# Two groups' affine, residual and norm moved from the last stage into the attention before it, and the folding of its weights moved into the experts

## Chip, cores and metric

The kernel runs on one core of a Trainium2 chip (trn2). The metric is the device time of one launch in microseconds; the time of a kernel is the median of its runs. The compute engines are TensorE (PE), VectorE (DVE), ScalarE (ACT) and GpSimd (POOL). SyncE (SP) issues most of the DMAs, ACT's queue the others.

## The reference, cut to what matters

A batch of sequences with 128 channels passes through four layers, each made of an attention-like mixer and a feed-forward part. In the kernel it is 32 tiles of 128 rows, held in `xt`, and worked on in eight groups of four tiles (`TG = 4`, `GT = 512` rows). Three parts matter here:

- the feed-forward part of layer 2: eight experts (gate, up, silu, down), of which each row takes the best two;
- the mixer of layer 3: four selective state-space (mamba) layers in a row, each with a projection, a short convolution, a recurrence over time with 16 states, a gate, a projection out, and a residual and normalisation behind it;
- the feed-forward part of layer 3: two layers of local attention with rotary positions and a gated MLP.

Between the last two stands the normalisation's affine and the outer residual, followed by the norm before the last part:

```
x = x_norm * w + b            # affine of the norm behind the mixer
x = x + x6                    # residual: what entered layer 3
x7 = x                        # residual of the last part
x = (x - mean(x)) / sqrt(var(x) + eps)
```

The convolution before the recurrence (4 taps) and the input projection are both linear, so the kernel multiplies the taps into the projection's matrix beforehand. This is the "folding": for each of the four layers a tile of 128 x 1024 taps times the projection (128 x 256, repeated four times).

## The kernel before, in words

The stages run one after another, each with its own pools: `l01`, `l2_attn`, `l2_ffn` (the experts), `l3_attn` (four mamba layers x eight groups = 32 items), `l3_ffn` (two layers x eight groups = 16 items).

**Who sets the order.** In `l2_ffn` the tile framework schedules the instructions by its own estimates. In `l3_attn` and `l3_ffn` nothing is issued while the code runs: a `Recorder` (L335) takes every operation with a key, which is its place in a written plan plus a shift for its kind; `Recorder.run` (L529) then does a list scheduling by a cost model of its own, with the smallest key first among what is ready, and issues the planned order, which is kept on each engine. An operation recorded in one stage can't be issued in another. All recorded operations bear line L299 in the profile, so they are told apart by their tiles.

**Folding (`ssm_fold`, L1511).** SP loads the taps (`cw`, one row broadcast to 128 partitions, 512 KB written) and the projection (`inx`, 128 KB), POOL multiplies. `l3_attn` (L1861) begins with four folds, one for each layer, each stored to a DRAM tile `wxd`, and then `weights(0)`, which loads the first layer's pack `w_L3a` (128 x 968) and reads its folded matrix back into `wx`. Both rings have two buffers; the weights of layer l+1 are loaded while the last group of layer l runs. The folds' operands and `w_L3a` go through SP's queue, behind the stores of `x6`.

**Items of the attention (`ssm_run`, L1758).** Item i is layer i/8, group i%8, with key origin `i * L`, `L = 32`. Per item POOL does eight multiplies of 128 x 2048 (`sb<-sw,sB`, the input of the scans), one of `sw`, two of `scq` and two operations of 128 x 512 for the norm (`xt<-so,smv` and `xt<-xt,srs`); DVE does 32 scans; PE transposes the results back and sums them over the states.

**The last stage (`l3_ffn`, L2072).** It loads its constants (`L3f`, `L3mask` on ACT's queue, `w_ln` on SP's), clears the parts of some tiles on POOL, and records 16 items with keys from `L3F` (L2162): `aff`, `hT`, `qkv`, `rot`, `tr`, `max`, `mn`, `sc`, `val` and the nine of `tail` (`wo` to `x`). For layer 0, `l3_affine` (L2206) does for each group what stands in the block above: SP loads `xo` (from `x6`), three operations on POOL (times w, plus b, plus `xo`), a store of `x7` on SP, statistics on DVE, Ln and Exp on ACT, and two more operations on POOL (minus mean, times 1/sigma). `l3_hT` transposes the result on PE, `l3_qkv` projects it with weights that are split into two parts: `l3_weights` (L2171) loads them in pieces (`w_in`, 128 x 512), ACT casts the upper part, POOL subtracts to get the rest (`wqkv_lo`, `w_lo`), and POOL then scales the rotary table `tab` from `w_L3f`.

`l3_affine` and the changed functions are in this listing.

Of the kernel before, what the change touches and what calls it, by code (L numbers as in the profile page):

```python
# [11 lines left out]
F32 = mybir.dt.float32  # L12
# [10 lines left out]
P = 128  # L23
NSEQ = 16
SEQ = 256
NTOK = NSEQ * SEQ
D = 128
# [629 lines left out]
class Ker:  # L657
    def __init__(self, ctx, tc, packs, dram, x_in, out):
        self.ctx, self.tc = ctx, tc
        self.nc = Engines(tc)  # L660
        self.packs, self.dram = packs, dram
        self.x_in, self.out = x_in, out
        nc = self.nc
        self.cp = ctx.enter_context(tc.tile_pool(name="cp", bufs=1))
        self.wp = ctx.enter_context(tc.tile_pool(name="wp", bufs=1))
        self.sp = self.sp0 = ctx.enter_context(tc.tile_pool(name="sp", bufs=2))

        self.xd = ctx.enter_context(tc.tile_pool(name="xd", bufs=1, space=bass.MemoryType.DRAM))
        self.x6 = self.xd.tile([P, NTOK // P, D], F32, name="x6")
        self.c = self.load("const")  # L670
        self.ident = self.cv("ident")
        self.xt = self.cp.tile([P, NTOK // P, D], F32, name="xt")
        xv = x_in.rearrange("b (k p) d -> p (b k) d", p=P)
        for g in range(4):
            s = slice(8 * g, 8 * g + 8)
            nc.sync.dma_start(self.xt[:, s], xv[:, s])

    def load(self, name, pool=None):
        pk = self.packs[name]
# [828 lines left out]
        r[0] += 1  # L1508
        return r[1][(r[0] - 1) % len(r[1])]

    def ssm_fold(self, tag, wx):  # L1511

        nc = self.nc
        t = self.ring("sb", [P, 4, GT], 7).rearrange("p n t -> p (n t)")
# [240 lines left out]
        ),  # L1755
    }

    def ssm_run(self, items, begin, norm, finish, N, after=None):  # L1758

        nq, n = N // 4, len(items)  # L1760
        L = 8 * nq
        pl = self.plan
        ev = []

        def at(t, f, *a):
            ev.append((t, len(ev), f, a))

        self.rec.shift = {k: pl["slot"] * v for k, v in pl["shift"].items()}

        for i, item in enumerate(items):  # L1770
# [12 lines left out]
            at(o + pl["src"], self.ssm_src, S)  # L1783
            if after:
                at(o + pl["src"] + 0.1, after, item)
            for c in range(2):
                at(o + pl["u"][c], self.ssm_in, S, c)
            for k in range(2):
                at(o + pl["z"][k], self.ssm_in, S, 2 + k)
            at(o + pl["silu"], self.ssm_silu, S)  # L1790
            at(o + pl["xp"], self.ssm_xp, S)
            for k in range(4):
                at(o + pl["dt"][k], self.ssm_dt, S, k % 2, k > 1)
            for k in range(3):
                at(o + pl["soft"][k], self.ssm_soft, S, k)
            for q in range(nq):
                s = o + 8 * q
                at(o + pl["bl"][q], self.ssm_bload, S, q)
                for c in range(2):
                    at(s + 4 * c + pl["b"][0], self.ssm_b, S, q, c)  # L1800
                for j in range(8):
                    at(s + j - 2.6, self.ssm_exp, S, q, j)
                    at(s + j, self.ssm_scan, S, q, j)
                    t = s + 9 + j
                    at(t + 0.2, self.ssm_tr, S, q, j)
                    at(t + 0.5, self.ssm_ev, S, q, j)
                    if j % 2:
                        at(t + 1.3, self.ssm_y, S, q, j // 2)
            e = o + L
            for k in range(2):  # L1810
                at(e + pl["ys"][k], self.ssm_ys, S, k)
                at(e + pl["gt"][k], self.ssm_gt, S, k)
            at(e + pl["out"], self.ssm_out, S)
            for t in pl["fin"]:
                at(e + t, step, "f", finish, item, S)
        ev.sort(key=lambda e: e[:2])
        for t, _, f, a in ev:
            self.rec.key, self.rec.kind = pl["slot"] * t, f.__name__[4:] or a[0]
            f(*a)
        self.nc.record(None)  # L1820
        self.rec.penalty = pl["pen"]
        self.rec.run(pl["ahead"])
        self.last_act = self.nc.scalar.last

    def l2_attn(self):
        nc, pk = self.nc, self.packs["L2a"]
        with ExitStack() as st:
# [9 lines left out]
            self.ssm_fold("L2", wx)  # L1837
            A, dd = self.ssm_decay(W, 8)
            b = self.sbank()
            for c in range(2):  # L1840
# [20 lines left out]
    def l3_attn(self):  # L1861
        nc = self.nc
        with ExitStack() as st:
# [3 lines left out]
            self.rec.apart, self.rec.switch, self.rec.rate = True, 0.09, 2330.0  # L1867
            self.rec.key = -1e6
            nc.record(self.rec)
            wd = self.dp.tile([4, P, 1024], F32, name="wxd", bufs=1)  # L1870
            for l in range(4):
                wx = self.ring("s4", [P, 2, GT], 2).rearrange("p a b -> p (a b)").rearrange("p (k e) -> p k e", k=4)
                self.ssm_fold(f"L3{l}", wx)
                nc.sync.dma_start(wd[l], wx.rearrange("p k e -> p (k e)"))
            cur = [self.xt[:, TG * g : TG * (g + 1)] for g in range(NG)]
            live = {}

            def weights(l):
                pk = self.packs[f"L3a{l}"]
                wt = self.ring("w_L3a", [P, pk.width], 2)  # L1880
                nc.sync.dma_start(wt, self.dram[f"L3a{l}"])
                wx = self.ring("wx", [P, 4, 256], 2)
                nc.sync.dma_start(wx.rearrange("p k e -> p (k e)"), wd[l])
                W = lambda n: pk.view(wt, n)
                live[l] = [W, wx]

# [16 lines left out]
            def after(item):  # L1903
                l, g = item
                if g == NG - 1 and l < 3:
                    weights(l + 1)

            weights(0)
            self.ssm_run([(l, g) for l in range(4) for g in range(NG)], begin, norm, finish, 16, after)


    def l2_ffn(self):
        nc, pk = self.nc, self.packs["L2m"]
        with self.tc.tile_pool(name="moe", bufs=2) as tp, self.tc.tile_pool(name="moew", bufs=1) as wp:
# [22 lines left out]
            for g in range(NG):  # L1937
                nxt = self.moe_route(g + 1, S[g + 1], W) if g + 1 < NG else none()
                prev = None
                for e in range(9):  # L1940
# [6 lines left out]
                    prev = (g, e, h, S[g], dw[e]) if e < 8 else None  # L1947
                    if e >= 2:
                        next(nxt, None)
                for _ in nxt:  # L1950
                    pass

# [119 lines left out]
    def l3_ffn(self):  # L2072
        nc = self.nc
        with ExitStack() as st:
# [5 lines left out]
            wm = self.load("L3mask", stat)  # L2080
            self.M = lambda n: self.packs["L3mask"].view(wm, n)
            self.wln = stat.tile([P, 2, D], F32, name="w_ln")
            nc.sync.dma_start(self.wln.rearrange("p a d -> p (a d)"), self.dram["L3ln"])
            self.epst = stat.tile([P, 1], F32, name="epst3")
            nc.vector.memset(self.epst, EPS)
            x7 = self.xd.tile([P, NTOK // P, D], F32, name="x7")
            ring = lambda n, f: [f(i) for i in range(n)]

            def shifted(i):
# [36 lines left out]
            for l in range(2):  # L2126
                at(pl["L"] * NG * l + pl["w"], "w", lambda l=l: live.update({l: self.l3_weights(l)}))
                for g in range(NG):
                    o = pl["L"] * (NG * l + g)
                    S = dict(i=NG * l + g, l=l, q=[], v=[], vx=[], live=live, xs=self.xt[:, TG * g : TG * (g + 1)])  # L2130
                    part = slice(TG * g, TG * (g + 1))
                    if l == 0:
                        at(o + pl["aff"], "aff", self.l3_affine, S, self.x6[:, part], x7[:, part])
                    at(o + pl["hT"], "hT", self.l3_hT, S)
                    for k in range(TG):
# [25 lines left out]

    L3F = dict(  # L2162
        L=46.0, w=-14.0, aff=-8.0, hT=4.0, qkv=8.0, tr=18.0, mid=(27.0, 41.0), tail=(66.0, 73.0, 75.0, 77.0, 81.0, 85.0, 88.0, 92.0, 96.0),
        pen=819.1, ahead=200.0, shift={
            "aff": -5.1, "gate": -11.4, "gelu": 394.9, "hT": -62.4, "ln": 137.7, "max": -127.7, "mn": -410.9,
            "nrm": 69.1, "qkv": -128.2, "rot": -171.0, "sc": 39.2, "stick": 33.1, "tr": -158.4, "up": 14.7,
            "val": -79.2, "w": 39.8, "w2": 358.8, "wo": -262.4, "x": 1.0, "yT": 26.4,
        },
    )

    def l3_weights(self, l):  # L2171
        nc = self.nc
        pk, p3 = self.packs[f"L3f{l}"], self.packs[f"L3w{l}"]
        wt = self.ring("w_L3f", [P, pk.width], 2)
        nc.sync.dma_start(wt, self.dram[f"L3f{l}"])
        parts = []
        for nm, bufs in (("wqkv", 1), ("w1", 2)):
            n = p3.items[nm][2][0]
# [2 lines left out]
            for j in range(0, n, 512):  # L2181
# [311 lines left out]
def kernel(ctx, tc, packs, dram, x_in, out, stages=STAGES):  # L2493
    k = Ker(ctx, tc, packs, dram, x_in, out)
    for s in stages:
        with tc.tile_pool(name="w_" + s, bufs=1) as k.wp, tc.tile_pool(name="ps_" + s, bufs=8, space=PSUM) as k.ps:
            k.nc.in_order(k.IN_ORDER.get(s, ""))
            getattr(k, s)()
    k.store()


# [19 lines left out]
```

## Time and profile before

| what | value |
|---|---|
| runs | 3915.74, 3921.61, 3924.74 us |
| median | 3921.61 us |
| the profiled execution's own time | 3928.12 us |
| its span in the profile | 3926.3 us |
| mean granted PE clock | 0.932 |
| PE busy | 3373.7 us (86%) |
| DVE busy | 3142.2 us (80%) |
| ACT busy | 2631.6 us (67%) |
| POOL busy | 2431.3 us (62%) |

The stages as the trace shows them: the experts from about 1318 to 1645 us, the attention of layer 3 from there to 3213, the last stage to the end at 3926. The experts take 39.7 us a group, the attention 46.8 us an item, the last stage 40.4 us an item.

The profile's second part cuts the span into 40 slices of 98 us; a digit is the busy share of an engine in tenths. PEclk is the clock that TensorE was granted, in tenths of its full rate. A line of a timeline gives start and busy time in us, the engine, the operation with its output and inputs, how many of them stand in a row, and in brackets how long the engine was idle before and what it waited for. In a table of windows each row is a stretch of time with the busy time of PE, PE's weight loads, DVE, ACT and POOL (the count of instructions in brackets), then the granted clock, the share of DMA time and GB/s.

### The profile page before, as it was taken

What the parts mean: (1) busy time and instruction counts of PE and PEld (TensorE: products, weight loads), DVE (VectorE), ACT (ScalarE), POOL (GpSimd) and SP (SyncE); (2) the same over time, 40 slices, a digit from 0 to 9 for tenths busy, and PEclk for the clock granted to TensorE, in tenths of its full rate; (3) what the DMA queues carried; (4) which work ended last, traced back from release to release, by engine and by line L of the source; (5) the groups of instructions that cost most, each with busy time, mean ns of one, the idle gap of its engine ahead of it and who ended that gap; (6) DMA issues with size and microseconds to landing.
All of it is one profiled execution on the core that took longest, in us unless ns stands there. A gap on an engine that the chain in (4) does not pass through costs nothing.

```text
span 3926.3 us, 77843 instructions
## 1 busy us (share of the span) xinstructions
PE 3373.7 (86%) x31425; PEld 2258.7 (58%) x31425; DVE 3142.2 (80%) x5420; ACT 2631.6 (67%) x4291; POOL 2431.3 (62%) x1163
## 2 busy tenths in 40 slices
PE   7863147666799899879999999999999968999998
PEld 4321034445355688736666666666666646777776
DVE  4699867556488677559999999999999968888874
ACT  4542024343587443369999999999999967777766
POOL 3454412211387200179999999999999978665553
PEclk9876568878899999899999999999999989999999
DMA  1012121321121100222222232222222220000001
GB/s 47 1 37 36 35 49 34 60 34 27 50 74 67 37 6 9 75 78 99 91 102 88 89 110 89 99 89 94 99 89 98 89 87 28 12 12 6 6 11 37
DMA packets 113833, 224.10 MB, mean 57 GB/s; under 512 B 53536, under 2 KB 84896, under 8 KB 94368
## 3 DMA queue, kind: packets, MB, share of 16 engines
q1 hardware_dynamic: 110736, 214.35, 17.8%
q8 instruction: 247, 4.05, 0.4%
q10 hardware_dynamic: 2736, 4.78, 0.4%
q14 instruction: 114, 0.93, 0.1%
HBM read 195.10 MB, written 21.76 MB: 55 GB/s over the span
## 4 chain that ended last, share of the span: by engine, by line
PE 46%; ACT 17%; DVE 4%; issue 2%; DMA 1%; POOL 1%; POOLq 0%; SPq 0%; DVEq 0%; ACTq 0%
PE spb L299 14%; PE fb L299 10%; PE shT L299 8%; ACT abuf L299 5%; ACT shs L299 5%; PE gu L299 5%; PE sy L299 4%; PE md L299 3%; PE fp L299 2%; ACT L299 2%; ACT su L299 2%; ACT s L299 1%; DVE mx L299 1%; PE mx L299 1%; DVE qr L299 1%
## 5 line engine op out<-in xcount | busy, mean ns | idle before, releaser
L299 POOL TENSOR_TENSOR sb<-sw,sB 128x2048 f32<-128x2048 f32 x288 | 1333.5, 4655 | 52.3 <-PE shT L299 49.8
L299 DVE TENSOR_TENSOR_SCAN sb<-abuf,sb 128x512 f32<-128x512 f32 x1152 | 1323.4, 1203 | 44.3 <-ACT abuf L299 22.9
L299 ACT ACTIVATE abuf<-sdl,sA 128x510 f32<-128x510 f32 x1152 | 780.9, 702 | 46.6 <-DVE sb L299 43.1
L299 PEld LDWEIGHTS shT<-w_const,sb 128*128 128x128 f32 x4608 | 595.0, 194 | 284.9 <-ACT shs L299 118.5
L299 PE MATMUL shT<-w_const,sb 128*128 128x128 f32 x4608 | 667.8, 283 | 29.6 <-ACT shs L299 16.0
L299 ACT COPY shs<-shT 128x512 f32<-128x512 f32 x920 | 517.7, 597 | 49.8 <-PE shT L299 35.4
L299 PE MATMUL sy<-shs,scq 128*32 128x256 f32 x4608 | 360.0, 390 | 0.2 <-DVE shs L299 0.2
L299 PE MATMUL spb<-ypad,wx 128*128 128x512 f32 x640 | 304.8, 613 | 6.1 <-ACT su L299 3.0
L299 DVE TENSOR_REDUCE mx<-fp 128x8 f32<-128x1024 f32 x160 | 193.7, 1218 | 105.9 <-PE fp L299 104.2
L299 POOL TENSOR_TENSOR qn<-qn,qr 128x512 f32<-128x512 f32 x128 | 163.8, 1281 | 172.6 <-DVE qr L299 114.9
L299 ACT ACTIVATE pt<-fp 128x1024 f32<-128x1024 f32 x96 | 97.2, 1024 | 181.8 <-PE fp L299 177.6
L299 ACT ACT_TABLE_LOAD x148 | 189.9, 1283 | 25.0 <-PE fb L299 18.2
L299 POOL TENSOR_TENSOR yn<-xt,nmv 128x512 f32<-128x512 f32 x23 | 24.0, 1043 | 285.8 <-DVE nmv L299 239.3
L299 PE MATMUL gu<-my,gu 128*128 128x512 f32 x768 | 197.6, 406 | 1.9 <-ACT gu L299 1.5
L299 PEld LDWEIGHTS spb<-ypad,wx 128*128 128x128 f32 x640 | 116.1, 194 | 142.6 <-issue 115.3
L299 ACT ACTIVATE mh<-gu,w_moe 128x512 f32<-128x512 f32 x128 | 88.2, 689 | 158.0 <-PE gu L299 135.6
L299 DVE COPY shs<-shT 128x512 f32<-128x512 f32 x232 | 152.4, 678 | 46.2 <-PE shT L299 31.0
L299 PE MATMUL fb<-wqkv_hi,hT 128*128 128x512 f32 x384 | 162.4, 441 | 4.5 <-ACT hT L299 1.3
L299 PEld LDWEIGHTS sy<-shs,scq 128*32 128x32 f32 x4608 | 100.2, 108 | 113.1 <-issue 44.7
L299 PEld LDWEIGHTS gu<-my,gu 128*128 128x128 f32 x768 | 140.9, 190 | 32.7 <-ACT gu L299 1.6
L299 POOL TENSOR_TENSOR g8k<-soft,gz 128x2048 f32<-128x2048 f32 x28 | 102.9, 3684 | 71.3 <-DVE gw L299 52.3
L299 PE MATMUL spb<-sxs,w_L3a 80*128 80x512 f32 x256 | 139.3, 626 | 7.0 <-DVE s L299 2.6
(377 smaller groups left out, 7172.6 us busy)
## 6 DMA issues: line engine op xcount, KB each, us to landing
sB<-scr SPq DMA_DIRECT2D x144, 1024.0 KB
l1scr<-qk SPq DMA_DIRECT2D x24, 256.0 KB
QS<-l1scr SPq DMA_DIRECT2D x96, 64.0 KB
KS<-l1scr SPq DMA_DIRECT2D x96, 64.0 KB
pks<-pk SPq DMA_DIRECT2D x4, 1152.0 KB
rec<-pks SPq DMA_DIRECT2D x8, 576.0 KB
x<-xt SPq DMA_DIRECT2D x16, 256.0 KB
xo<-x SPq DMA_DIRECT2D x16, 256.0 KB
```

The lines of the kernel that those rows point to most:

```text
L299: r = f(*a, **kw)
```

## The change

It has five parts.

1. The folding and the first layer's weights go into the experts' stage. A pool `held` is opened before `l2_ffn` and closed behind `l3_attn`; it holds `w_L3a` and `wx` of layer 0. After expert 4 of group 0, 1, 2 and 3 the fold of layer 0, 1, 2 and 3 is written into `l2_ffn` (for layer 0 the load of `w_L3a` too), through `fold_in` and `fold_out` with one buffer each; layers 1 to 3 go to `wxd` as before. `l3_attn` then has nothing to fold, and layer 0 nothing to load.
2. `ssm_run` gets a hook `end`: for the last layer's groups 0 and 1 it records `l3_affine` with the keys `n * L + 1` and `n * L + 2`, that is, at the end of the plan of `l3_attn`. `w_ln` is loaded for it in that stage. `x7` is made at the start.
3. `l3_ffn` leaves `aff` out for the groups that have had it.
4. In `l3_ffn` `w_ln` is loaded on ACT's queue, and `w_L3f` behind the pieces of `wqkv`.
5. `L3F` has another `pen`, `ahead` and other shifts.

```diff
+        self.x6, self.x7 = (self.xd.tile([P, NTOK // P, D], F32, name=n) for n in ("x6", "x7"))
+        self.affined = set()
...
+    def hold(self):
+        self.held = ExitStack()
+        p = self.held.enter_context(self.tc.tile_pool(name="held", bufs=1))
+        self.held_w = p.tile([P, self.packs["L3a0"].width], F32, name="w_L3a_h")
+        self.held_x = p.tile([P, 4, 256], F32, name="wx_h")
+        self.wd = self.xd.tile([4, P, 1024], F32, name="wxd")
+        self.folded = set()
+
+    def fold(self, l, t, wx):
+        nc = self.nc
+        if not l:
+            nc.sync.dma_start(self.held_w, self.dram["L3a0"])
+        self.ssm_fold(f"L3{l}", wx if l else self.held_x, t)
+        if l:
+            nc.sync.dma_start(self.wd[l], wx.rearrange("p k e -> p (k e)"))
+        self.folded.add(l)
...
@@ ssm_run
+            if end and i < n - NG + 2 and i >= n - NG:
+                at(n * L + 1.0 + i - n + NG, self.ssm_end, end, item)
@@ l3_attn
-            wd = self.dp.tile([4, P, 1024], F32, name="wxd", bufs=1)
-            for l in range(4):
+            for l in sorted(set(range(4)) - self.folded):
                 wx = self.ring("s4", [P, 2, GT], 2).rearrange("p a b -> p (a b)").rearrange("p (k e) -> p k e", k=4)
-                self.ssm_fold(f"L3{l}", wx)
-                nc.sync.dma_start(wd[l], wx.rearrange("p k e -> p (k e)"))
+                self.fold(l, self.ring("sb", [P, 4, GT], 7).rearrange("p n t -> p (n t)"), wx)
+            self.ring("w_L3a", [P, self.packs["L3a0"].width], 1)
+            self.ring("wx", [P, 4, 256], 1)
+            for nm, t in (("w_L3a", self.held_w), ("wx", self.held_x)):
+                self.rings[nm] = [0, [t] + self.rings[nm][1]]
...
+            self.wln = self.stat.tile([P, 2, D], F32, name="w_ln4")
+            nc.sync.dma_start(self.wln.rearrange("p a d -> p (a d)"), self.dram["L3ln"])
+
+            def end(item):
+                g = item[1]
+                part = slice(TG * g, TG * (g + 1))
+                self.l3_affine(dict(xs=self.xt[:, part]), self.x6[:, part], self.x7[:, part])
+                self.affined.add(g)
@@ l2_ffn
+                    if e == 4 and g < 4:
+                        ft = wp.tile([P, 1280], F32, name="fold_in", bufs=1)
+                        self.fold(g, ft, wp.tile([P, 4, 256], F32, name="fold_out", bufs=1))
@@ l3_ffn
-            nc.sync.dma_start(self.wln.rearrange("p a d -> p (a d)"), self.dram["L3ln"])
+            nc.scalar.dma_start(self.wln.rearrange("p a d -> p (a d)"), self.dram["L3ln"])
-                    if l == 0:
+                    if l == 0 and g not in self.affined:
                         at(o + pl["aff"], "aff", self.l3_affine, S, self.x6[:, part], x7[:, part])
@@ L3F
-        pen=819.1, ahead=200.0, shift={
-            "aff": -5.1, "gate": -11.4, "gelu": 394.9, "hT": -62.4, "ln": 137.7, "max": -127.7, "mn": -410.9,
-            "nrm": 69.1, "qkv": -128.2, "rot": -171.0, "sc": 39.2, "stick": 33.1, "tr": -158.4, "up": 14.7,
-            "val": -79.2, "w": 39.8, "w2": 358.8, "wo": -262.4, "x": 1.0, "yT": 26.4,
+        pen=505.2, ahead=178.0, shift={
+            "aff": 36.5, "gate": 16.1, "gelu": 498.3, "hT": -76.4, "ln": 96.6, "max": -100.6, "mn": -467.4, "nrm": 45.2,
+            "qkv": -122.9, "rot": -191.8, "sc": 27.2, "stick": 43.1, "tr": -157.5, "up": 26.4, "val": -84.6, "w": 57.6,
+            "w2": 422.8, "wo": -123.9, "x": 203.0, "yT": 71.8,
@@ l3_weights
-        wt = self.ring("w_L3f", [P, pk.width], 2)
-        nc.sync.dma_start(wt, self.dram[f"L3f{l}"])
...
+            if nm == "wqkv":
+                wt = self.ring("w_L3f", [P, pk.width], 2)
+                nc.sync.dma_start(wt, self.dram[f"L3f{l}"])
```

The written place of a fold (group g, expert 4) is not where it ends up: the framework's schedule puts all four among the experts of group 0 and ahead of group 1's routing on SP and POOL.

More of the change, by code (lines that the diff above doesn't have):

```diff
@@ L668, in __init__ @@
         self.xd = ctx.enter_context(tc.tile_pool(name="xd", bufs=1, space=bass.MemoryType.DRAM))
-        self.x6 = self.xd.tile([P, NTOK // P, D], F32, name="x6")
+        self.x6, self.x7 = (self.xd.tile([P, NTOK // P, D], F32, name=n) for n in ("x6", "x7"))
+        self.affined = set()
         self.c = self.load("const")
@@ L676, in __init__ @@
             nc.sync.dma_start(self.xt[:, s], xv[:, s])
+    held = None
+    def hold(self):
[13 more added lines that the diff above has]
+        self.folded.add(l)
     def load(self, name, pool=None):
@@ L1509, in ring, with ssm_fold @@
         return r[1][(r[0] - 1) % len(r[1])]
-    def ssm_fold(self, tag, wx):
+    def ssm_fold(self, tag, wx, t):
         nc = self.nc
-        t = self.ring("sb", [P, 4, GT], 7).rearrange("p n t -> p (n t)")
         o = self.packs["cw"].items[tag][1]
@@ L1756, with ssm_end, ssm_run @@
     }
-    def ssm_run(self, items, begin, norm, finish, N, after=None):
+    def ssm_end(self, end, item):
+        end(item)
+    def ssm_run(self, items, begin, norm, finish, N, after=None, end=None):
         nq, n = N // 4, len(items)
@@ L1836, in l2_attn @@
             wx = self.stat.tile([P, 4, 256], F32, name="wx")
-            self.ssm_fold("L2", wx)
+            self.ssm_fold("L2", wx, self.ring("sb", [P, 4, GT], 7).rearrange("p n t -> p (n t)"))
             A, dd = self.ssm_decay(W, 8)
@@ L1880, in weights @@
                 wt = self.ring("w_L3a", [P, pk.width], 2)
-                nc.sync.dma_start(wt, self.dram[f"L3a{l}"])
                 wx = self.ring("wx", [P, 4, 256], 2)
-                nc.sync.dma_start(wx.rearrange("p k e -> p (k e)"), wd[l])
+                if l:
+                    nc.sync.dma_start(wt, self.dram[f"L3a{l}"])
+                    nc.sync.dma_start(wx.rearrange("p k e -> p (k e)"), self.wd[l])
                 W = lambda n: pk.view(wt, n)
@@ L1906, in after @@
                     weights(l + 1)
+            self.wln = self.stat.tile([P, 2, D], F32, name="w_ln4")
[5 more added lines that the diff above has]
+                self.affined.add(g)
             weights(0)
-            self.ssm_run([(l, g) for l in range(4) for g in range(NG)], begin, norm, finish, 16, after)
+            self.ssm_run([(l, g) for l in range(4) for g in range(NG)], begin, norm, finish, 16, after, end)
     def l2_ffn(self):
@@ L2082, in l3_ffn @@
             self.wln = stat.tile([P, 2, D], F32, name="w_ln")
-            nc.sync.dma_start(self.wln.rearrange("p a d -> p (a d)"), self.dram["L3ln"])
+            nc.scalar.dma_start(self.wln.rearrange("p a d -> p (a d)"), self.dram["L3ln"])
             self.epst = stat.tile([P, 1], F32, name="epst3")
             nc.vector.memset(self.epst, EPS)
-            x7 = self.xd.tile([P, NTOK // P, D], F32, name="x7")
+            x7 = self.x7
             ring = lambda n, f: [f(i) for i in range(n)]
@@ L2495 @@
     for s in stages:
+        if s in ("l2_ffn", "l3_attn") and not k.held:
+            k.hold()
         with tc.tile_pool(name="w_" + s, bufs=1) as k.wp, tc.tile_pool(name="ps_" + s, bufs=8, space=PSUM) as k.ps:
@@ L2498 @@
             getattr(k, s)()
+        if s == "l3_attn":
+            k.held.close()
     k.store()
```

## The prediction

> **What bounds the kernel now.** I read the page's slices first, then the chain of waits, then timelines at the three places which the change touches.
>
> ```profile
> span 3926.3 us, 77843 instructions
> ...
> PE   7863147666799899879999999999999968999998
> ...
> POOL 3454412211387200179999999999999978665553
> PEclk9876568878899999899999999999999989999999
> ```
>
> Where PE shows 9 the end is set by PE with POOL, at 9 too through the attention, close behind; an edit pays there only if it takes work off PE. The dents are where waits decide: slices 17 and 18 (8 and 7: attention of layer 3 begins) and 33 and 34 (6 and 8: last stage begins). The chain through the first dent:
>
> ```profile
> 1645.71 5.06 DMA sb<-in_cw_dram
> ...
> 1650.78 6.64 DMA w_L3a<-in_L3a_dram
> ...
> 1657.53 0.23 ACT sA L299
> ...
> 1658.17 0.48 ACT ypad L299
> ...
> 1664.12 5.14 PE spb L299 x8
> ```
> ```profile
> 1657.53 0.23 ACT L299 ACTIVATE sA<-w_L3a 128x32 f32<-128x32 f32 x1 [15.74 <-DMA w_L3a<-in_L3a_dram]
> ```
>
> Loads of the fold's operands, then w_L3a, then ACT's preparation, then three more evictions and the first projections. ACT sat 15.74 us, while group 0's transposes had been done since 1645.34+0.63. POOL and PE around the second dent (start, busy us, engine, work, wait):
>
> ```profile
> 3176.24 9.39 POOL L299 TENSOR_TENSOR sb<-sw,sB 128x2048 f32<-128x2048 f32 x2
> 3194.39 2.08 POOL L299 TENSOR_TENSOR xt<-so,smv 128x512 f32<-128x512 f32 x2 [8.76 <-DVE smv L299]
> ...
> 3216.38 6.14 POOL L299 TENSOR_TENSOR xt<-xt,w_ln 128x512 f32<-128x512 f32 x5 [0.80 <-DMA w_ln<-in_L3ln_dram]
> 3222.48 1.26 POOL L299 TENSOR_TENSOR xt<-xt,xo 128x512 f32<-128x512 f32 x1
> 3223.70 2.49 POOL L299 TENSOR_TENSOR wqkv_lo<-w_in,wqkv_hi 128x512 fp32r<-128x512 f32 x2
> 3226.14 1.69 POOL L299 TENSOR_TENSOR tab<-w_L3f,w_L3f 128x128 f32<-128x128 f32 x4
> 3227.79 1.26 POOL L299 TENSOR_TENSOR xt<-xt,xo 128x512 f32<-128x512 f32 x1
> ```
> ```profile
> 3233.55 1.11 PE L299 MATMUL fb<-w_const,xt 128*128 128x128 f32 x4 [24.24 <-POOL xt L299]
> 3235.93 0.79 PE L299 MATMUL fb<-wqkv_hi,hT 128*128 128x512 f32 x1 [1.26 <-ACT hT L299]
> ```
> ```profile
> 3213.00:3233.00 20.00, 0.00 (x0) 0.00 (x0) 2.36 (x17) 4.44 (x9) 19.03 (x28) 0.51 0.65 212
> 3484.93:3525.34 40.41, 40.07 (x731) 31.87 (x732) 34.49 (x73) 31.27 (x59) 26.22 (x24) 1.00 0.08 22
> ```
>
> After the last normalisation (3212.49+1.04) POOL works through affine operations, weight remainders (wqkv_lo) and tables; PE stands 24.24 us, busy 0 of 20. Behind that the last stage runs at 40.41 us an item with PE busy 40.07.
>
> **The change part by part.** The sum is made on the profiled execution: span 3926.3, its own time 3928.12, the runs' median 3921.61. A difference in the span is carried to the median unchanged.
>
> *A, expert front.* The built order puts group 0's exp and a table load ahead of the first two weight casts on ACT. Before, the cast ran at 1322.88 and the exp (0.23) and load (1.28) from 1323.41. So the first cast comes up to 1.5 later, of which the load's 1.28 was waited for anyway by the first silu at 1325.80; I take +1.1. SP now issues w_L3a, cw and inx ahead of the weights of experts 2 and 3: some 1.1 MB, at the 335 GB/s of 1646 to 1658 3.4 us; the first twelve gu matmuls (5.62 us) cover it, 0, at worst 3.4. Four folds of 2.32 (half of 4.64, POOL 1651.43) join POOL. The first two fit in its idle pieces of 1.83, 2.98 and 3.22 us between the experts' remainders. The last two stand between the last expert's remainder and group 1's meq, where POOL paused 8.05:
>
> ```profile
> 1345.50 1.30 POOL L299 TENSOR_TENSOR gu<-w_in,gu 128x512 fp32r<-128x512 f32 x1 [2.50 <-ACT gu L299]
> 1354.84 0.73 POOL L299 TENSOR_TENSOR meq<-meq,w_moe 128x256 f32<-128x256 f32 x1 [8.05 <-DVE meq L299]
> ```
>
> The pause would hold both multiplies, but fold_in has one buffer, so each takes a load (5.06 in the chain) and a multiply, 7.4. If the second fold ends near 1340, by expert 5's remainder, the fourth ends between 1355 and 1358, an estimate; group 1's meq is queued behind it on POOL, and DVE's mrk, with the hidden products queued behind that, waits for meq. meq is 0 to 3.2 late; four gu banks hold 1.5 of it, I take +0.9. The wxd stores stand on SP between these loads. A is +2 (0 to +7).
>
> *B, attention start.* Eight loads on SP, four stores, the multiplies and the wait for w_L3a leave. ACT was free since 1641.8 (table load 1640.51+1.28), so the first ypad copy comes behind the transposes, 1646.05, not 1658.08: −12.0. What is late next is the pitch of transposes and copies through one bank (1.8 each), unchanged. If a fold straggles, 3 us come back: −9.
>
> The eight first projections took 5.13, the next eight 3.70; the granted clock was 0.50 in 1658 to 1664, though PE was busy 3.35 of those 6 us with transposes, and 0.90 in the next 16. So I leave the 1.4 us of a cold start as they are; without them −13.4. [...]
>
> *C, attention tail.* Ten affine and norm operations come onto POOL among its last four to five items: twice three of 1.26 and two of 1.05, 11.8 us. POOL's pauses there are one an item, 1.54 before 3069.84 and 3.12 before 3117.17, none after; about 4.1 of them absorb, leaving 7.7 ahead of the last sb multiplies (end 3185.63). DVE's last four scans start at 3188.7, so POOL is 3.0 ahead: +4.7 (0 if the multiplies are taken first, +9 if the xo loads or the store x7 on SP, ahead of the last item's scr stores, add a wait).
>
> *D, junction.* Groups 0 and 1 need no affine there. PE's transposes can start at once; the first qkv matmul needs wqkv_hi (cast 3220.66, its load unchanged) and wqkv_lo. POOL's order is memsets (to 3215.6), five w_ln operations (6.14), two wqkv_lo (2.49), tab, two xo adds, then qn; w_ln is third on ACT's queue instead of first on SP's. If it lands as before (2.8 after issue) the second wqkv_lo ends at 3225.0 and the first qkv at 3225.3, −10.6 against 3235.93. Three more microseconds for its place in the queue give −7.6. Remainders moved among the first qn operations (2.6 to 3.3 on POOL) may give back as much, −4.3. I take −8, near the row where w_ln is the releaser.
>
> *E, inside the last stage.* The new keys and shifts reorder 16 items. Item pitch is PE's (40.07 of 40.41). Counted in the built orders, changes of tile shape on PE fall from 351 to 317, at about 0.1 each −3.5. PE idled some 17 us in 3233 to 3433 and 15 after 3833; less POOL work at the start and one MLP fewer behind the last wo may save a little, −2.5. No row shows the new order: −14 to +6, taken −6.
>
> Sum: +2 − 12.0 + 4.7 − 8 − 6 = −19.3, span 3907.0, median 3902.
>
> **Rivals.** 0.2% of the time, about what a measurement here can tell, is 7.8 us: 3913.8 and 3929.4 bound "same".
> *R1, given back.* POOL, full in the tail, pays the whole of what it saves at the junction: C +9.2, D −4.3, E 0, so 2 − 12 + 9.2 − 4.3 = −5, 3916.5. For: POOL's 100% in 3160 to 3180, one store on SP ahead of scr. Against: 3.0 us of lead, pauses until 3117. It includes the case that the early loads still make ACT wait. Chance 0.17, most of it "same".
> *R2, slower.* One mechanism: the last stage's new keys add one wait to each item, p us where PE is now 40.07 of 40.41 busy; 16p against −13.3 from A to D. Break-even is at 0.83, slower beyond 0.2% from 1.3; at 2 us +18.7, 3940. For: the shifts of wo (+138) and x (+202) move far, PE has only 0.3 of slack. Against: fewer shape changes, same work. Chance 0.07.
> *R3, all hidden.* A +1, B −13.4, C 0, D −10.6, E −10: −33, 3888.6. For: POOL chain is free of waits at the junction; pauses in the tail. Chance 0.15.
>
> **How the numbers follow.** Forecast 0.61 (own range 3894 to 3912), R1 0.17 (0.05 of it faster), R2 0.07, R3 0.15. Faster 0.61+0.05+0.15 = 0.81, same 0.12, slower 0.07. The range runs from R3's time less 2.6 to R1's plus 1.5, 3886 to 3918; outside lie R2, the far halves of R3's and R1's bounds.
>
> **What would show it.** In the profile after: first ypad copy about 12 us nearer to the last expert matmul, ACT without a w_L3a wait (B); meq of group 1 less than 3.2 us late, POOL busy with folds of 2.3 (A); the attention's last sb multiply about 8 later against its start, last scans 5 later (C); PE's gap of 24.24 down to 12 to 16, first qkv 8 to 11 nearer to the last norm (D); item pitch 40.0 to 40.4 (E). The forecast is wrong if the tail lengthens by over 9, if the gap stays above 20, or if an item takes 41 or more.

## The result, and the profile after

The changed kernel takes 3941.33 us (median of five, 3938.49 to 3947.67) against 3921.61: ratio 1.0054, interval 1.0040 to 1.0068. The forecast was 3902 and faster; it is 20 us slower. One execution was profiled, span 3936.7; the figures below are from it.

```profile
span 3936.7 us, 77807 instructions
...
PE   7862247577799899889999999999999878999998
...
POOL 3455313211587200099999999999999968655552
PEclk8886578788899999999999999999999989999999
```

Slices 18 and 33 rose by one each, where the two dents were; slice 32, the attention's tail, fell from 9 to 8. Cut at five events that both traces have, the spans give this (us):

| stretch | before | after | difference |
|---|---|---|---|
| experts' first `myT` copy to the attention's first `ypad` copy | 337.8 | 328.1 | −9.7 |
| to the second to last pair of `scq` on POOL | 1432.5 | 1432.1 | −0.4 |
| to the attention's end (first memset of the last stage) | 123.0 | 137.4 | +14.4 |
| to the first `wqkv_lo` matmul | 22.9 | 14.8 | −8.1 |
| to the end | 689.8 | 712.5 | +22.7 |

The sum is +18.9. What lies before the experts has the same order in both kernels and differed by 8.5 us between these two executions, so it is left out; the medians differ by 19.7. Below, "the last stretch" is the table's last row, and "pitch" is the time from one item to the next.

**Attention start** (PE's timeline). The transposes come right behind the last expert and the projections 6.2 us later, with no load in between.

```profile
1639.18 0.63 PE L299 MATMUL spb<-w_const,xt 128*128 128x128 f32 x4 [1.31 <-DVE xt L299]
1640.49 0.66 PE L299 MATMUL spb<-w_const,xt 128*128 128x128 f32 x4 [0.67 <-ACT ypad L299]
...
1645.40 5.21 PE L299 MATMUL spb<-ypad,wx_h 128*128 128x512 f32 x8 [0.67 <-ACT ypad L299]
1651.38 3.70 PE L299 MATMUL spb<-ypad,wx_h 128*128 128x512 f32 x8 [0.78 <-ACT su L299]
```

**Attention tail** (POOL's timeline, and a window). Affine operations stand between the `sb` multiplies of the last two items, the last item's `sw` then waits for `sdl`, and for 18 us PE is busy for 11.27 at a clock of 0.53.

```profile
3107.70 1.28 POOL L299 TENSOR_TENSOR xt<-xt,xo 128x512 f32<-128x512 f32 x1
...
3117.87 1.05 POOL L299 TENSOR_TENSOR xt<-xt,ln_mv 128x512 f32<-128x512 f32 x1
...
3122.98 1.04 POOL L299 TENSOR_TENSOR xt<-xt,srs 128x512 f32<-128x512 f32 x1
3127.05 2.35 POOL L299 TENSOR_TENSOR sw<-sdl,su 128x1024 f32<-128x1024 f32 x1 [3.02 <-DVE sdl L299]
3129.36 3.78 POOL L299 TENSOR_TENSOR scq<-scc,dmask 128x1024 f32<-128x1024 f32 x2
3135.04 9.05 POOL L299 TENSOR_TENSOR sb<-sw,sB 128x2048 f32<-128x2048 f32 x2 [1.90 <-PE shT L299]
...
3161.44 18.12 POOL L299 TENSOR_TENSOR sb<-sw,sB 128x2048 f32<-128x2048 f32 x4
```
```profile
3112.00:3130.00 18.00, 11.27 (x22) 4.98 (x23) 17.86 (x25) 11.69 (x18) 14.90 (x10) 0.53 0.18 64
```

**Junction** (POOL and PE). `w_ln` landed 7.4 us after the end of the attention's last operation on POOL (3209.34), not 2.8; five affine operations and the weight remainders queue behind it, and PE's first `wqkv_lo` matmul waits for them.

```profile
3216.75 6.14 POOL L299 TENSOR_TENSOR xt<-xt,w_ln 128x512 f32<-128x512 f32 x5 [5.37 <-DMA w_ln<-in_L3ln_dram]
3222.86 2.50 POOL L299 TENSOR_TENSOR wqkv_lo<-w_in,wqkv_hi 128x512 fp32r<-128x512 f32 x2
```
```profile
3216.22 0.76 PE L299 MATMUL fb<-wqkv_hi,hT 128*128 128x512 f32 x1 [9.16 <-DMA w_ln<-in_L3ln_dram]
3224.17 0.79 PE L299 MATMUL fb<-wqkv_lo,hT 128*128 128x512 f32 x1 [7.18 <-POOL wqkv_lo L299]
```

**Last stage** (a window of two items, and the chain of waits in one of them). Two items take 83.80, 41.9 each, and PE is busy 79.97 of that: as much work as before, with more waiting. In every second item the chain runs through the DMA that shifts the rows by one, `sh<-xt`, 9.16 us, straight to the statistics that DVE makes of it (`st`) and on to PE.

```profile
3481.70:3565.50 83.80, 79.97 (x1461) 64.43 (x1460) 67.38 (x141) 62.47 (x117) 49.25 (x48) 1.00 0.05 13
```
```profile
3546.49 0.70 DVE xt L299
...
3547.21 9.16 DMA sh<-xt
...
3556.40 0.22 DVE st L299
...
3560.57 0.41 PE fb L299 x2
```

The whole last stretch, first before and then after, as a window and as DVE's waits for this DMA (us in total, times, the longest). PE stood idle 34.3 us of it before and 54.8 after. DVE waited for the shift in both kernels. Before, the four waits lie at the ends of the stage (0.63 and 1.30 in the first two items, 4.20 and 3.37 in the last two), with none in the steady items; of the ten after, five, of 1.0 to 1.5, lie in every second steady item.

```profile
3236.52:3926.30 689.78, 655.49 (x11676) 517.27 (x11674) 544.83 (x1178) 486.52 (x901) 400.90 (x383) 0.99 0.06 17
3224.17:3936.70 712.53, 657.71 (x11671) 524.83 (x11671) 536.61 (x1160) 494.00 (x916) 400.35 (x386) 0.97 0.06 17
```
```profile
DVE st L299 <- DMA sh<-xt: 9.5, 4, 4.2
DVE st L299 <- DMA sh<-xt: 19.6, 10, 5.4
```

### The profile page after: what moved, and what is told of

Its sections match the earlier page's. It is cut to its first block, busy times and chain, and to the rows that moved or that the text cites. A ratio compares the mean times of both kernels' runs of the same rounds, so it can differ in the third digit from the quotient of the medians.

```text
span 3936.7 us, 77807 instructions
## 1 busy us (share of the span) xinstructions
PE 3373.9 (86%) x31425; PEld 2263.4 (57%) x31425; DVE 3142.4 (80%) x5414; ACT 2636.0 (67%) x4297; POOL 2404.2 (61%) x1163
## 4 chain that ended last, share of the span: by engine, by line
PE 45%; ACT 16%; DVE 3%; DMA 3%; issue 2%; POOL 1%; SPq 0%; POOLq 0%; ACTq 0%; DVEq 0%
PE spb L299 14%; PE shT L299 9%; PE fb L299 8%; ACT abuf L299 5%; PE sy L299 4%; ACT shs L299 4%; PE gu L299 4%; PE md L299 3%; DMA sh<-xt 2%; PE fp L299 2%; ACT L299 2%; ACT su L299 1%; ACT s L299 1%; ACT h L299 1%; DVE sb L299 1%
## 5 line engine op out<-in xcount | busy, mean ns | idle before, releaser
L299 POOL TENSOR_TENSOR sb<-sw,sB 128x2048 f32<-128x2048 f32 x288 | 1307.1, 4558 | 72.2 <-PE shT L299 60.9
L299 ACT ACTIVATE abuf<-sdl,sA 128x510 f32<-128x510 f32 x1152 | 779.9, 700 | 54.8 <-DVE sb L299 50.8
L299 PE MATMUL spb<-ypad,wx 128*128 128x512 f32 x384 | 181.9, 606 | 1.6 <-ACT su L299 0.9
L299 POOL TENSOR_TENSOR qn<-qn,nr 128x512 f32<-128x512 f32 x128 | 130.9, 1044 | 27.5 <-ACT nr L299 27.3
L299 POOL TENSOR_TENSOR sw<-sdl,su 128x1024 f32<-128x1024 f32 x40 | 95.1, 2376 | 73.9 <-DVE sdl L299 60.3
```

Of the source, the lines that this page charges most:

```text
L299: r = f(*a, **kw)
```

## Experiments

Ratios are to the kernel before on the same chip; the times of stretches are from each kernel's profile, cut as in the table.

**e1, e2: are it the new numbers of `L3F`?** e1 puts the old numbers into the changed kernel, e2 the new ones into the kernel before.

```diff
-        pen=505.2, ahead=178.0, shift={"aff": 36.5, ...
+        pen=819.1, ahead=200.0, shift={"aff": -5.1, ...
```

> The changed kernel with the last stage's old numbers (pen, ahead and all shifts of L3F as before); everything else as changed. Theory 1, the new numbers cost the last stage its pitch: from the first wqkv_lo matmul to the end the changed kernel took 712.5 us against 689.8, so this one gives back about 22.7: 3919 us (3913 to 3925), pitch of steady items back at 40.4. Theory 2, the pitch is lost because the first two groups come without their affine and the items start out of step: it stays at 41.9 an item and 3941 us (3936 to 3946).

> The kernel before with the new numbers of L3F and nothing else. Theory 1: slower by about 22.7 in the last stage alone, 3944 us (3936 to 3952). Theory 2, the numbers fit only the new start, or do not matter: 3922 us (3916 to 3928) with a pitch of 40.4.

e1: 4020.61 us, 1.0254 (1.0241 to 1.0267). e2: 4002.04, 1.0198 (1.0185 to 1.0211). Both theories miss. The old numbers on the new list of operations cost 79 more than the new ones, the new numbers on the old list 80 more than the old. In e1 the late items take 51 us, and PE's longest wait in each of them is one of 4.0 for ACT's `sq` (waits of PE over four items, then a window of one item):

```profile
PE fb L299 <- ACT sq L299: 16.1, 4, 4.0
```
```profile
3734.90:3785.90 51.00, 43.70 (x738) 33.86 (x731) 35.69 (x74) 29.28 (x54) 21.76 (x21) 0.93 0.02 5
```

So numbers and list of operations are a pair: with two groups' affine taken away, the list scheduling makes another order out of the same numbers, and it waits elsewhere. Neither kernel shows what the other's numbers "cost".

**e3: the folds alone.** The changed kernel without the hook `end`, with the last stage as before.

```diff
-            self.ssm_run([...], begin, norm, finish, 16, after, end)
+            self.ssm_run([...], begin, norm, finish, 16, after)
```

> Only the folds and layer 0's weights moved into the experts; no affine in the attention, last stage as before. From the experts' first myT copy to the attention's first ypad copy the changed kernel took 328.0 us against 337.8. If that gain is kept through the attention: 3912 us (3909 to 3916). Rival, an early start is lost again in the attention's queue of loads: 3922 us (3918 to 3926).

3914.88 us, 0.9982 (0.9971 to 0.9992). First stretch 328.9 (−8.9), last 689.2 (−0.6): the gain of parts A and B is real and kept, less 2.1 in the steady attention.

**e4: the affine late in the attention's plan.** As e1 with one line more.

```diff
-                at(n * L + 1.0 + i - n + NG, self.ssm_end, end, item)
+                at(n * L + 120.0 + i - n + NG, self.ssm_end, end, item)
```

> As e1_old_keys, with the affine's keys 120 instead of 1 behind the plan's end, so that POOL's planned order has six of the ten operations behind the attention's last eleven sb multiplies or in its pauses, and the last item's sw and scq ahead of them. Theory 3, the attention's tail got 14.4 us longer (122.9 to 137.3 from the second to last scq pair to the end) because the ten operations, 11.8 us, stand on POOL ahead of the last item's multiplies: 8 to 13 us less than e1_old_keys. Rival, the tail is set by DVE's scans or by the last item's front on ACT, whatever POOL does: within 3 us of e1_old_keys.

4010.07 us, 1.0226 (1.0213 to 1.0239), 10.5 less than e1. The tail took 125.7 against e1's 138.6. POOL's order decides the tail: four of the ten operations now stand behind the last multiplies, and the last item's `sw` waits 0.41, not 3.02.

**f1, f2: the old plan, with the two groups' affine taken out after planning.** The last stage has its old loads and numbers and records all eight affines; those of groups 0 and 1 are planned and not issued. f1 has key 120 in the attention, f2 key 1.

```diff
-            for eng, name, a, kw in ops[i].calls:
+            for eng, name, a, kw in () if ops[i].skip else ops[i].calls:
```

> The change's folds, the affine with key 120 in the attention, the last stage's loads and numbers as before, and its plan made as before with all eight affines recorded, of which those of groups 0 and 1 are then not issued: PE's planned order of the last stage is that of before. Theory 4, the last stage loses only where its plan is made anew for other operations, not because two groups are ready earlier: folds -9.3, tail +2.7 (123.0 to 125.7 with key 120), first wqkv_lo matmul 9 to 13 us earlier against the attention's end, rest of the stage 689 to 694: 3904 us (3900 to 3909). Theory 2, groups that are ready earlier put the items out of step: rest over 705, 3918 us or more.

> As f1_old_plan_late with the change's own keys (1 behind the plan's end) for the affine in the attention. Theory 3, ten operations on POOL ahead of the last item's multiplies cost the tail 14.4 instead of 2.7: 10 to 13 us over f1_old_plan_late, 3916 us (3911 to 3921). Rival, the junction gives it back, since the norms stand earlier: within 3 us of f1_old_plan_late.

f1: 3908.11 us, 0.9963 (0.9950 to 0.9975). f2: 3922.81, 1.0004 (0.9995 to 1.0013). In f1 the last stretch took 688.7 and an item 40.40 with PE busy 40.06 (window):

```profile
3466.40:3506.80 40.40, 40.06 (x732) 31.86 (x732) 34.48 (x73) 31.27 (x59) 26.43 (x26) 1.00 0.08 22
```

Groups that are ready earlier do no harm; the loss comes with the plan made anew. f2's tail is 138.4 against f1's 125.7, 12.7 where e4 had 12.9; its time is 14.7 over f1 and 2 above the range that was expected. The junction was overestimated: first `wqkv_lo` matmul 14.7 after the attention's end, 8.2 earlier than before and not 9 to 13, since the old order keeps two casts of later weight chunks ahead of those of `hT` on ACT.

**f3, f4: `w_ln`.** f3 puts its load back on SP's queue in the changed kernel; f4 is f1 with `w_ln` loaded once at the start and `w_L3f` behind the `wqkv` pieces.

```diff
-            nc.scalar.dma_start(self.wln..., self.dram["L3ln"])
+            nc.sync.dma_start(self.wln..., self.dram["L3ln"])
```

> The changed kernel with w_ln's load back on SP's queue, nothing else. In the changed kernel w_ln landed 7.4 us after the attention's end (2.8 before), and five affine operations and two weight remainders stand behind it on POOL. Theory 5, the queue costs the junction 4 to 5 us: 3937 us (3934 to 3940). Rival, the time is decided later in the stage: 3941 us (3938 to 3944).

> As f1_old_plan_late, but w_L3f is loaded behind the wqkv pieces as in the change, and w_ln is loaded once at the kernel's start and kept, so that nothing at the junction waits for it. In the changed kernel the weight casts came 5.0 us after the attention's end, 7.1 before. Theory 5: 2 to 3 us less than f1_old_plan_late, 3902 us (3897 to 3907). Rival, the first qn on POOL sets the start of the stage: the same as f1_old_plan_late within 1.5.

f3: 3935.34 us, 1.0034 (1.0022 to 1.0046), 6.0 less than the changed kernel. `w_ln` landed 2.7 after the attention's end (3207.04), and the first `wqkv_lo` matmul came after 10.2, not 14.8 (POOL):

```profile
3209.78 6.17 POOL L299 TENSOR_TENSOR xt<-xt,w_ln 128x512 f32<-128x512 f32 x5 [0.75 <-DMA w_ln<-in_L3ln_dram]
3215.90 2.50 POOL L299 TENSOR_TENSOR wqkv_lo<-w_in,wqkv_hi 128x512 fp32r<-128x512 f32 x2
```

f4: 3906.95, 0.9953 (0.9938 to 0.9969); 1.2 from f1, which its interval doesn't tell from none, and less than the 2 to 3 expected. In its profile the junction is 1.5 shorter (13.2), and the last stretch is 690.4.

**g1, g2: the shift's DMA cut in half.** The planned order stays as it was; two of the four tiles are not shifted.

```diff
-            nc.sync.dma_start(sv[1:P], xs[0 : P - 1, :, 64:128])
+            nc.sync.dma_start(sv[1:P, 0:2], xs[0 : P - 1, 0:2, 64:128])
```

> The changed kernel with its planned order, but the DMA sh<-xt that shifts the rows by one copies two of the four tiles of a group (254 pieces of 256 bytes instead of 508; the other two tiles' shifted half is zero, so that this part of the computation is left out). In the changed kernel this DMA stands on the chain of the steady items with 9.16 us from the end of xt to DVE's statistics, and DVE waits 1.2 us for it in every second item. Theory 6, the plan has no slack behind this DMA and the pitch of 41.9 is its latency: pitch at or below 41.0, rest of the stage 12 to 16 less, 3927 us (3923 to 3932). Rival, the pitch comes from the evictions on ACT that PE waits for: pitch 41.9, 3941 us (3937 to 3945).

> The kernel before with the same cut of sh<-xt (its last item's order moves a little too). DVE never waits for this DMA there. Theory 6: pitch 40.4 as it was, 3920 us (3916 to 3924). Rival, the DMA's descriptors cost every plan the same: 10 or more below 3920.

g1: 3926.62 us, 1.0011 (1.0000 to 1.0022), 14.7 less than the changed kernel; last stretch 698.2, 14.3 less. g2: 3926.70, 1.0014 (1.0004 to 1.0025); pitch 40.4 as before. Its last stretch is 3.7 longer, behind the last item's first `qn`, where its order had moved, and its time lies above the range that was expected. That DVE never waits for this DMA in the kernel before, as the expectation of g2 says, holds for the steady items alone; the four waits at the ends are gone in g2, and up to the 13th item its statistics come 2 to 3 us earlier after the first `wqkv_lo` matmul than before. In g1 DVE waits for the shift only once more, 1.69 us at 3885.95. In the steady item below its statistics follow two reductions without a wait, 8.0 us after the end of `xt` (3552.48), where the changed kernel has 9.2:

```profile
3551.79 0.69 DVE L299 TENSOR_TENSOR xt<-fb,xt 128x512 f32<-128x512 f32 x1 [3.69 <-PE fb L299]
...
3560.52 0.60 DVE L299 BATCH_NORM_STATS2 st<-sh 128x6 f32<-128x64 f32 x4
```

So leaving out half of this DMA is worth 14.3 us in the new order. That is not its share of the 22.7, since the old order waits for it too. To the statistics of the 13th item the new order is 21.6 behind the old one (584.0 and 562.4 after the first `wqkv_lo` matmul), and with the half shift in both it is still 14.2 behind (573.7 in g1, 559.5 in g2): about a third of the lag up to there goes with the DMA. The pitch came down only to 41.3 (82.7 for two items), where 41.0 or less was expected. The rest of the gain is at both ends of the stage.

**h1, h2: new plans with a whole-row shift.** Other numbers for the new list, chosen among plans in which DMAs were counted 1 to 2 us later; the shift moves whole rows to have fewer pieces, which makes it twice the bytes. Both also have key 120, `w_ln` kept from the start and one buffer for `xo`.

```diff
-            nc.sync.dma_start(sv[1:P], xs[0 : P - 1, :, 64:128])
+            nc.sync.dma_start(sv[1:P], xs[0 : P - 1])
```

> A third plan for the last stage, made for the new operations (groups 0 and 1 without their affine): other numbers in L3F, chosen among plans executed with every DMA of the stage counted 1 to 2 us later than the Recorder counts it; the shift sh<-xt moves whole rows (127 pieces of 2 KB instead of 508 of 256 bytes), xo has one buffer, the affine has key 120 and w_ln is kept from the start. Theory 6, what the changed kernel's plan lacked is slack behind this DMA: a pitch of 40.4 to 41.2 from the first steady item on, DVE waits for sh gone, 3905 us (3895 to 3915). Rival, any plan made anew leaves waits that the Recorder does not count: pitch over 41.5, 3920 us or more.

> As h1_new_plan_slack with a second set of numbers, found from another start and kept for a shorter start of the stage. Theory 6: 3908 us (3898 to 3918). Rival: 3920 us or more.

h1: 3993.85 us, 1.0165 (1.0151 to 1.0180). h2: 3951.29, 1.0054 (1.0040 to 1.0068). Both miss by far, and they don't test what they were made for: the whole-row shift is slower, not faster. In h2, from its issue on SP to the statistics that wait for it went 13.0 us (9.2 in the changed kernel), at a DMA share of 0.08, which is 1.3 of sixteen engines (SP, DVE, and a window of the time between):

```profile
3451.32 1.24 SPq L299 DMA_DIRECT2D sh<-xt  x2
```
```profile
3464.37 0.66 DVE L299 BATCH_NORM_STATS2 st<-sh 128x6 f32<-128x64 f32 x4 [0.27 <-DMA sh<-xt]
```
```profile
3453.00:3464.00 11.00, 10.81 (x146) 7.96 (x135) 10.80 (x23) 7.28 (x16) 8.37 (x8) 1.00 0.08 26
```

DVE waited six times for it in h1 between 3450 and 3750, 23.5 us in all.

**i1, i2, i3: a plan that counts the shift as the trace shows it.** i1 and i2 have the narrow shift, key 120, `w_ln` kept, the Recorder's cost of the shift corrected, and two sets of numbers searched under that; i3 has the same repairs with the changed kernel's own numbers and costs.

```diff
+            if self.switch and out.ap[0][1] == P - 1:
+                return 6.5, 9.2
-        pen=505.2, ahead=178.0, shift={"aff": 36.5, ...
+        pen=1625.0, ahead=369.5, shift={"aff": -71.1, ...
```

> The change with key 120 for the affine, w_ln kept from the start, the old narrow shift, and a plan made anew for the new operations: the Recorder counts the shift's DMA with 6.5 us on SP's queue and 9.2 to landing, as the trace of the changed kernel shows them (it counted 3.0 and about 7.3), and L3F has other numbers, searched under that. Theory 6, the changed kernel's plan lost because it counted this DMA too short: pitch at or below 40.6, from the attention's end to the kernel's end at most 703 us (f4_w_ln_kept took 703.6), 3900 us (3888 to 3908). Rival, a plan made anew carries other waits that the Recorder does not see: over 715 us there, 3918 us or more.

> As i1_plan_counts_shift with a second set of numbers from another start of the search. Theory 6: 3904 us (3892 to 3912). Rival: 3918 us or more.

> The changed kernel with its own numbers and plan, only with key 120 for the affine and w_ln kept from the start. If the terms add: 3941.3, less 12.8 for the tail and 5 to 6 for w_ln: 3923 us (3919 to 3927). Rival, an earlier start of the stage is lost again in its pitch: 3930 us or more.

i1: 3901.70 us, 0.9944 (0.9930 to 0.9958). i2: 3898.31, 0.9937 (0.9925 to 0.9950). i3: 3921.40, 1.0001 (0.9990 to 1.0013). The terms of i3 add as expected, and what is left between it and i2, 23.1, is the last stage's plan: last stretch 711.1 in i3, 680.9 in i2 (the two profiled executions lie further apart than the medians). f4 shows the same with the old plan: it issues what i3 issues, and its last stretch is 690.4. In i2 almost nothing is left to wait for in the steady items (window, 250 us):

```profile
3480.00:3730.00 250.00, 249.14 (x4461) 197.26 (x4463) 201.48 (x430) 191.64 (x358) 141.26 (x135) 1.00 0.03 7
```

i2 beats the kernel before by 23.5 us and the changed one by 43.0.

**j1, j2: the whole shift, made faster.** j1 is the changed kernel with its order on every engine, j2 is i2's kernel; in both the 127 rows go as 112 and 15.

```diff
-            nc.sync.dma_start(sv[1:P], xs[0 : P - 1, :, 64:128])
+            nc.sync.dma_start(sv[1:113], xs[0:112, :, 64:128])
+            nc.sync.dma_start(sv[113:P], xs[112 : P - 1, :, 64:128])
```

> The changed kernel, its order on every engine kept and the whole computation done, with the shift's 127 rows as two DMAs of 112 and 15 rows. In h2 the shift of 127 rows ran at a DMA share of 0.07, one of sixteen engines. Theory 6: the DMA's latency is the loss; if it falls from 9.2 to 8 us or less, the last stretch falls from 712.5 to 697 to 704, 3928 us (3923 to 3934). Rival, what g1 gained it gained by moving half the bytes and issuing half the pieces on SP, which stays: latency 9 us or more, 3941 us (3937 to 3945). [...]

> The kernel of i2_plan_counts_shift2 with the same split, its order kept. Its plan has room for 9.2 us: nothing changes in the steady items; at the stage's end, where little other work is left, up to 5 us less: 3896 us (3891 to 3900). Rival, one more DMA for each item on SP delays what stands behind it: 3901 us or more.

j1: 3926.59 us, 1.0013 (1.0004 to 1.0022), 14.7 less than the changed kernel with the whole computation done; last stretch 696.2, 16.3 less, with PE idle 44.6 of it. The three DMAs of a shift (the last one carries two rows across the tiles' edges) left SP in 2.32 us, where two had taken 7.28, and the statistics stand where DVE gets to them, without a wait anywhere in the stage (SP, then DVE):

```profile
3546.17 2.32 SPq L299 DMA_DIRECT2D sh<-xt  x3
```
```profile
3554.18 0.59 DVE L299 BATCH_NORM_STATS2 st<-sh 128x6 f32<-128x64 f32 x4
```

j2: 3898.11, 0.9936 (0.9920 to 0.9951), the same as i2 (3898.31): where the plan has the room, as here, the faster transfer was worth nothing that the intervals tell.

## Why the prediction was wrong, step by step

- **A, expert front: right.** From the `myT` copy to PE's first transposes of the attention 325.1 before and 327.4 after: +2.3, predicted +2. In other runs with the folds it was up to 330.3, +5.2, still inside 0 to +7. DVE's `meq` of group 1 ended at 1347.98, POOL took it up at 1350.64 behind the fourth fold, 2.7 late, inside the 0 to 3.2.
- **B, attention start: right.** From those transposes to the first `ypad` copy 12.74 and 0.67: −12.1, predicted −12.0. The cold start stayed, as taken: eight projections in 5.21, the next eight in 3.70. PE had worked at full clock until the last expert (1.00 from 1320 to 1639) and from 1360 on never paused over 1.31 us, but for 6 us it did only transposes; the granted clock was 0.71 in 1639.0 to 1645.4 and 0.71 in the first eight projections. What brought it down is not shown: PE was busy in only 3.52 of the 6.40 us to 1645.4, and no run here tells the transposes from the pauses between them.
- **C, attention tail: mis-sized.** Predicted +4.7 of 0 to 9, measured +14.4. Two deductions failed: 4.1 for POOL's pauses and 3.0 for its lead over DVE. From the second to last pair of `scq` to the end of the last `sb` multiply went 95.0 us before and 107.6 after, +12.6 where 7.7 was predicted: POOL's pauses in it took up nothing and grew from 3.5 to 6.9, the wait for `sdl` (3.02) among them. From there to the attention's end it was 1.8 more, so the lead saved nothing either. Here a pause on an engine that waits for another was not free room. The shift of key from 1 to 120 gave 12.9 and 12.7 of the 14.4 back (e4, f2 against f1).
- **D, junction: right in sum, by luck.** Predicted −8, measured −8.1. f3 shows its inner term: the queue change of `w_ln` cost 4.6, where 0 to 3 had been allowed. Without it f3 has −12.7, and the prediction had −10.6: two errors of about 2 us cancelled.
- **E, inside the last stage: the step that failed.** Predicted −6 (−14 to +6), measured +22.7. It counted changes of tile shape in the built order (351 to 317), took a faster PE from that at about 0.1 us each (in the trace before, the matmul behind such a change starts 0.32 after a `wqkv_hi` matmul, 3523.37 to 3523.69, and 0.23 after one without a change, 3523.14 to 3523.37), and put no new wait into its sum. PE's busy time did not change (3373.7 and 3373.9 over the span); PE's idle time in the last stretch rose by 20.5, from 34.3 to 54.8. One of the new waits is known. Before, 14.0 us lay between the shift's issue and its statistics, 4.8 more than it needs; in the new order 9.2, nothing to spare, in every second item (SP and DVE, before and then after):

```profile
3501.21 7.27 SPq L299 DMA_DIRECT2D sh<-xt  x2
3515.25 0.60 DVE L299 BATCH_NORM_STATS2 st<-sh 128x6 f32<-128x64 f32 x4
```
```profile
3547.21 7.28 SPq L299 DMA_DIRECT2D sh<-xt  x2
3556.40 0.66 DVE L299 BATCH_NORM_STATS2 st<-sh 128x6 f32<-128x64 f32 x4 [1.09 <-DMA sh<-xt]
```

  The profile before could have warned of it: no steady item waits for this DMA there, but the first two and the last two do, 9.5 us in all, and the prediction named none of them. The rival R2 had the mechanism (a wait per item, up to 2 us) at a chance of 0.07; the place that was found is not wo or x but the DMA between wo and the statistics.

What is shown: the loss goes with the plan and not with the earlier groups or the loads (f1; f4 against i3); 16.3 us of the last stretch go when this DMA alone is made faster under the new order (j1; 14.3 in g1); plans that count it as measured lose nothing (i1, i2). Not shown is that the DMA is most of the loss. DVE's waits for it grew by 10.1 us, from 9.5 to 19.6, and a faster shift would help the old order as well (g2, up to the 13th item), which no run tried to the end. With no wait for it at all, j1 still has a pitch of 41.3 (82.6 for two items) and 10.3 us more idle PE than before; these waits were not traced. Nor do j1 and g1 tell the DMA's latency from the time that it holds SP's queue, which they shorten together. i1 and i2 have other numbers too, so they don't show what the corrected cost alone does.

## What to carry to other kernels

A plan made anew is a new schedule, however small the edit: here the same work came out about 80 us slower with the partner's numbers (e1, e2). Before trusting a new plan, look in the old trace for the transfers that the order hides in its steady part and waits for at its ends, compare each one's measured time with the one that the planner counts, and ask how much room the new order leaves. Numbers that were searched for one list of operations mean nothing for another; to test a moved piece by itself, keep the old plan and leave the pieces out when it is issued. Work that was put on a nearly full engine cost its whole time here (11.8 us on POOL, the tail 14.4 longer), and 12.7 to 12.9 of it came back when its place in the order was later (e4, f1).

## What the runs showed of the hardware

- The shift of 127 rows (508 pieces of 256 bytes, SBUF to SBUF) held SP's queue for 7.3 us with its small companion and took 9.2 to its reader. As 127 pieces of 2 KB, twice the bytes, it took 13.0 at a DMA share of 0.08. As 112 and 15 rows it left SP in 2.32 and was read without a wait 8.0 us after `xt`, with bytes and pieces as in the first case: there the split of the rows alone made the difference.
- The DMA share was 0.08 in h2 (3453 to 3464), 1.3 of sixteen engines. In j1 it was 0.26 from 3546.2 to 3548 and 0.17 in the microsecond after, where the changed kernel's shift shows 0.14 at most in any microsecond from 3547 to 3557. So more engines were busy at once with the split (0.26 is 4.2 of sixteen); why the split does that, no run shows.
- A clock that the experts had kept at 1.00 was 0.71 on average over 6.4 us of transposes without a pause over 1.31 us (PE busy 3.52 of them), 0.50 from 1642 to 1648, 0.53 in the half microsecond after, and 1.00 again from 1648.5 on, 3.1 us into the projections.
